# Two graph layers on one core: the order of the steps from a list scheduler in the kernel's text in place of a table of offsets

## The chip, the core and the metric

The kernel runs on one core of a Trainium2 chip. Its time is the device time of one execution in microseconds (us), as the median of several runs. The core has TensorE (PE: matmuls; PEld is its weight load), VectorE (DVE), ScalarE (ACT), GpSimd (POOL) and SyncE (SP, which here only issues transfers). Every engine takes its own instructions strictly in the order in which the program lists them; semaphores make it wait for others. Sixteen DMA engines carry the transfers that SP and ACT issue.

## The reference

128 graphs of 128 nodes with 512 features go through two layers, each with a residual. All is float32.

```python
def _layernorm(x, axis=-1, eps=1e-5): ...
# layer 0: h = relu(layernorm(x)); x = x + GAT(h, adj)
feats = jnp.einsum('bnf,hfu->bhnu', X, W)              # 8 heads of 64
e_self, e_neigh = ...                                   # feats . a_self, feats . a_neigh
dense = leaky_relu(e_self[..., :, None] + e_neigh[..., None, :], 0.2)
dense = dense + NEG_BIG * (1.0 - A[:, None, :, :])
att = softmax(dense); out = relu(att @ feats + b)
# layer 1: h = relu(layernorm(x)); x = x + HG(h, adj)
#   hypergraph_conv: H = (adj != 0); out = Dn * (H @ (Be * (H^T @ (x @ W^T)))) + b
h1 = relu(hypergraph_conv(x, adj, W1, b1))              # 512 -> 1024
y = hypergraph_conv(layer_norm(h1, gamma, beta), adj, W2, b2) + x    # 1024 -> 512
```

## The kernel before

Work is cut into **steps**, each a Python function that issues a few instructions on one engine. Attention and the first product with the graph's matrix go graph by graph (`parts`); the two dense products of layer 1 go by pairs of graphs (`second`), since each takes seven half-size products in place of eight (u1 to u7 and v1 to v7, with sums us1..4, vs1..4 of halves on POOL, L789 to L837).

A graph's path: x.load (SP), statistics and relu (DVE, POOL, ACT: L433 to L462), a transposition `x`, features `f` (PE, L578), neighbour scores sent to DRAM and fetched back as a broadcast (`ed`, L618 to L636), leaky, mask, row maximum and exponentials (`sc`, `pp`, L638 to L670), a transposition `p`, `av` (PE, L672), `oT` (ACT, L686), a transposition `o`, scaling and addition (L695 to L707), again statistics and relu (`h1`), `z` (PE, L714), `zT` (ACT). Then for the pair: u products into PSUM banks ux and uy, kept by DVE into aL, aR, bL, bR (L840 to L873), relu into `r`, statistics (L751, `sq`), a transposition `r`, v products into vx and vy, kept by DVE into `v`, and for each graph `y` (PE, L918), `y.keep` (DVE, L925, writes xt) and the store.

A **transposition** takes three steps. `send` (L472) is a transfer from ACT's queue to DRAM, `fetch` (L481) four transfers on SP's queue back in blocks (tiles xm, pm, om, rm), and `turn` (L494) one DVE transpose of 32 x 32 blocks (L509). In the first graphs (`DIRECT`: 4 of x, p, o, 2 of r) it is four or eight PE transposes into a PSUM bank and a copy instead (L502 to L507).

What sets the **order**: `Order` (L150) holds every step at a place, and `issue` calls them sorted by it. The place is `origin(n) + AT[step] - sooner`: AT gives each step an offset, origin goes up by STEP = 19.25 per graph after the eight rows of EARLY, and EARLY and LATE move groups of steps of the first eight and last six graphs. W2_AT places the setup steps (weights, bias rows, sums of weight blocks). For instance `ra.fetch` is at 130.27, `ra.turn` at 133.81, `u7.keep` at 99.35 of the next pair (137.85 on the same scale), `u4` at 99.48.

Each tile comes from a pool with a number of buffers per tag. PSUM has 8 banks: two shared "ps" (z, av, k, y), two for f, one each ux, uy, vx, vy. SBUF tiles with one buffer are xn, hT, pp, pT, oT, o, h1; xt has 12.

Of the kernel before, what the change touches and what calls it, by code (L numbers as in the profile page):

```python
# [13 lines left out]
P = 128  # L14
# [7 lines left out]
STEP = 19.25  # L22
EARLY = (
    (0, 3.05, 1.85, 0.05, 1.85, 1.85, 1.53, 1.85, -6.41),
    (19.25, 0, 0.01, -0.36, -0.36, -0.36, -0.36, -0.36, -1.29),
    (39.4, 0, -3.95, 0, 0, 12.9, 12.9, 12.9, 17.9),
    (57.75, 0, 0, 0, 0.34, 0, 0, 0, 0),
    (77.73, 0, 0, 0, 0, -4.29, -4.29, -4.29, -4.29),
    (96.25, 0, -2.95, 0, 0, 0, 0.05, 0, 0),
    (115.45, 0, 0, 0, 0, 0, 10.16, 11.08, 11.08),  # L30
    (134.75, 0, 24.41, 0, 0, 0, 0, 0, 0),
)
LATE = (
    (0, 0, 0, 0, 1.89, 0, 0, 0),
    (0, 0, 0, 0, 0, 0, 0, 0),
    (0.25, 0, 0, 1.08, 1.08, 1.08, 1.08, 0.74),
    (0, 0.14, 0.14, 0.14, 0.26, 0.14, 0.14, 0.14),
    (0, 0, 0, 0, -0.72, 0.07, -0.72, 0.34),
    (0, 3.7, 0, 0, 0, 0, -3.96, -3.96),
)  # L40
AT = {
    "x.load": -19.25,
    "x.stats": -15.55,
    "x.mean": -14.6,
    "x.rstd": -14.03,
    "x.relu": -13.05,
    "x.send": -12.05,
    "x.fetch": -9.3,
    "x.turn": -3.58,
    "f": 0,  # L50
    "e": 2.18,
    "f.keep": 5.65,
    "e.send": 4.8,
    "e.fetch": 8.85,
    "d.leaky": 11.65,
    "d.leaky1": 12.71,
    "d.mask": 12.49,
    "d.mask1": 14.25,
    "d.max": 14.4,
    "d.max1": 15.7,  # L60
    "d.exp": 15.25,
    "d.exp1": 17.1,
    "p.send": 19.43,
    "p.fetch": 24.45,
    "p.turn": 29.56,
    "av": 33.41,
    "av.keep": 34.48,
    "o.send": 39.2,
    "o.fetch": 51.02,
    "o.turn": 55.26,  # L70
    "o.scale": 56.16,
    "o.add": 56.52,
    "h.stats": 58.76,
    "h.mean": 59.09,
    "h.rstd": 59.72,
    "h.relu": 62.32,
    "z": 71.55,
    "z.keep": 78.03,
    "h.add": 64.28,
    "mask.load": -17.62,  # L80
    "mask": -12.02,
    "adj.load": 25.02,
    "adj.turn": 29.78,
    "adj.weigh": 31.52,
    "k": 40.72,
    "k.keep": 42.52,
    "k.deg": 43.62,
    "us1": 80.14,
    "us2": 83.46,
    "us3": 86.28,  # L90
    "us4": 91.36,
    "u1": 81.64,
    "u1.keep": 84.95,
    "u6": 86.88,
    "u6.keep": 88.66,
    "u2": 88.99,
    "u2.keep": 91.33,
    "r.aL": 96.5,
    "u5": 94.53,
    "u7": 92.8,  # L100
    "u7.keep": 99.35,
    "r.bR": 101.65,
    "u4": 99.48,
    "u4.keep": 104,
    "r.bL": 106.21,
    "u3": 100.3,
    "u3.keep": 102.03,
    "r.aR": 102.79,
    "rb.send": 110.98,
    "rb.stats": 119.65,  # L110
    "rb.root": 125.09,
    "rb.fetch": 114.54,
    "rb.turn": 119.23,
    "ra.send": 107.42,
    "ra.stats": 126.05,
    "ra.root": 128.88,
    "ra.fetch": 130.27,
    "ra.turn": 133.81,
    "vs1": 123.44,
    "vs2": 138.14,  # L120
    "vs3": 137.02,
    "vs4": 154.95,
    "v1": 142.38,
    "v1.keep": 145.34,
    "a1": 146.75,
    "b1": 150.3,
    "b0": 152.19,
    "v6": 144,
    "v6.keep": 147.65,
    "v2": 146.6,  # L130
    "v2.keep": 149.75,
    "v5": 150.87,
    "v7": 149.88,
    "v7.keep": 152.5,
    "v4": 159.95,
    "v4.keep": 162.65,
    "v3": 161.6,
    "v3.keep": 163.6,
    "ya": 164.91,
    "ya.keep": 166.04,  # L140
    "ya.store": 169.02,
    "yb": 183.16,
    "yb.keep": 186.01,
    "yb.store": 186.48,
}
W2_AT = (36.61, 3.95, -8.22, 41.62, 45.15, 53.53, 54.68, 1.33, 71.89, 0.13, 2.77, 7.82, -19.26, -18.51, 0.66, 4.2, -4.88, -5.39)
DIRECT = {"x": 4, "p": 4, "o": 4, "r": 2}


class Order:  # L150

    def __init__(self):
        self.todo = []

    def at(self, place, fn, *args):
        self.todo.append((round(place, 3), len(self.todo), fn, args))

    def issue(self):  # L160
        for _, _, fn, args in sorted(self.todo, key=lambda t: t[:2]):
            fn(*args)
# [3 lines left out]
def gat_then_hypergraph_kernel(  # L166
# [31 lines left out]
    io = ctx.enter_context(tc.tile_pool(name="io", bufs=12))  # L198
    wk = ctx.enter_context(tc.tile_pool(name="wk", bufs=2))
    dr = ctx.enter_context(tc.tile_pool(name="dr", bufs=2, space=bass.MemoryType.DRAM))  # L200
    gp = ctx.enter_context(tc.tile_pool(name="gp", bufs=2))
    sm = ctx.enter_context(tc.tile_pool(name="sm", bufs=4))
    ps = ctx.enter_context(tc.tile_pool(name="ps", bufs=2, space=bass.MemoryType.PSUM))
    pv = ctx.enter_context(tc.tile_pool(name="pv", bufs=1, space=bass.MemoryType.PSUM))
    pa = ctx.enter_context(tc.tile_pool(name="pa", bufs=1, space=bass.MemoryType.PSUM))
    ctx.enter_context(tc.manual_schedule())

    def psum(name):
        return ps.tile([P, 512], F32, tag="ps", name=name)

    def psum2(name):
        return pa.tile([P, 2, 512], F32, tag="pa", name=name)

    def psum_sums(tag, name):
        return pv.tile([P, 512], F32, tag=tag, name=name)

# [6 lines left out]
    nc.gpsimd.memset(eps_col, EPS)  # L223

    S = [dict() for _ in range(N)]
    SP = [dict() for _ in range(N // G)]

    def load_x(n):
        S[n]["xt"] = io.tile([P, F], F32, tag="xt", name=f"xt_{n}")
        nc.sync.dma_start(S[n]["xt"], x[n])  # L230

    def load_mask(g):
        s = SP[g]
        s["at"] = gp.tile([P, G, P], F32, tag="at", name=f"at_{g}")
        nc.sync.dma_start(s["at"], adj[g * G : (g + 1) * G].rearrange("n c e -> c n e"))

    def load_adj(g):
        s = SP[g]
        pair = adj[g * G : (g + 1) * G]
        s["am"] = gp.tile([P, G * NB, B], F32, tag="am", name=f"am_{g}")  # L240
        for b in range(NB):
            nc.sync.dma_start(
                s["am"][b * B : (b + 1) * B],
                pair[:, :, b * B : (b + 1) * B].rearrange("n (a x) y -> x (n a) y", x=B),
            )

        s["hmb"] = gp.tile([P, G, P + 1], F32, tag="hmb", name=f"hmb_{g}")
        nc.sync.dma_start(s["hmb"][:, :, P], pair[:, 0, :].rearrange("n e -> e n"))

    t1, t2, t4 = (const.tile([P, KP, FV], F32, name=f"w2_t{i}") for i in (1, 2, 4))
    gb = const.tile([2 * KH, P], F32, name="gb")
    rows = {}
    for key, v, tile_, at in (
        ("a_self", a_self, t1, 0),
        ("a_neigh", a_neigh, t1, F),
        ("b0", b0, t2, 0),
        ("b2", b2, t2, F),
        ("b1", b1, t4, 0),  # L260
    ):
        flat = v.rearrange("h u -> (h u)") if len(v.shape) == 2 else v
        row = tile_[0:1].rearrange("o k c -> o (k c)")
        rows[key] = row[:, at : at + flat.shape[0]]
        nc.scalar.dma_start(rows[key], flat.unsqueeze(0))
    w0_sb = const.tile([P, KF, 2, FB + E], F32, name="w0_sb")
    we_sb = const.tile([P, KF, 2, E], F32, name="we_sb")
    w1_sb = const.tile([P, KF, DH], F32, name="w1_sb")
    w2_sb = const.tile([P, KH, F], F32, name="w2_sb")

    def load_w0(k):
        for b in range(2):
            nc.sync.dma_start(
                w0_sb[:, k, b, 0:FB].rearrange("p (h u) -> p h u", h=HB),
                w0[b * HB : (b + 1) * HB, k * P : (k + 1) * P, :].rearrange(
                    "h p u -> p h u"
                ),
            )

    def load_w1():  # L280
        sw["w1"] = True
        nc.sync.dma_start(w1_sb, w1t.rearrange("(k p) h -> p k h", p=P))

    def load_w2():
        sw["w2"] = True
        nc.sync.dma_start(gb[0:KH], gamma.rearrange("(k p) -> k p", p=P))
        nc.sync.dma_start(gb[KH : 2 * KH], beta.rearrange("(k p) -> k p", p=P))
        nc.sync.dma_start(w2_sb, w2t.rearrange("(k p) o -> p k o", p=P))

    sw = {}  # L290
    ones = const.tile([1, P], F32, name="ones")
    nc.vector.memset(ones, 1.0)
    b0_bc = const.tile([P, F], F32, name="b0_bc")
    b1_bc = const.tile([P, DH], F32, name="b1_bc")
    b2_bc = const.tile([P, F], F32, name="b2_bc")
    bw_bc = const.tile([P, F], F32, name="bw_bc")
    gbT = const.tile([P, 2 * KH], F32, name="gbT")
    a_bc = [psum_sums(tag, f"a_bc_{tag}") for tag in ("ux", "vx")]
# [479 lines left out]

# [405 lines left out]
```

## Time and profile before

| what | value |
|---|---|
| time, median of 3 runs (lowest, highest) | 2631.27 us (2630.47, 2631.73) |
| profiled execution: its span, the only time the page gives of it | 2656.0 us, 24.7 above the median |
| DMA | 553.44 MB, 208 GB/s; 16 engines busy 73% in the middle |
| PE idle 0 to 200 us, 200 to 2550, 2550 to 2656 | 59.0, 92.8, 11.6 us |
| k of pair 3, k of pair 63 (PE) | 180.47, 2554.76 us |
| u1 of pair 0; last f | 119.84; 2535.44 to 2539 us |
| transfers, median from issue to landing | xm 3.1, pm 2.9, om 2.0, rm 3.0, sc 3.8 us |

A profile line of instructions reads: line and engine, operation, out<-in by the program's names, count; then busy us and ns of one; then the engine's idle time just before and what ended it. A line of waits reads: who waited for whom, us in all, times, longest. The busy row has one digit for each fortieth of the span, 9 for 90% or more; PEclk is the clock granted to TensorE in tenths. A timeline row begins with its start and its length.

### The profile page before, as it was taken

To read this page: it belongs to the slowest core of one execution; us is meant where nothing else is said; L and a number is where in the kernel's file an instruction comes from. 1 tells how busy PE (TensorE), PEld (TensorE's weight loads), DVE (VectorE), ACT (ScalarE), POOL (GpSimd) and SP (SyncE) were. 2 spreads that over 40 slices of the span, in tenths; PEclk is the share of its full clock that TensorE was granted. 3 is DMA by queue.
4 is the path that set the end of the run, shared out by engine and by line. 5 is a ranking of instruction groups with operands and counts; after the bars stand their busy time and mean duration, and the time that the engine had idled before them with its cause. 6 is when DMAs were issued, how large, how long until landed. Compare 5 with 4: busy or idle time off the path is not lost. (4 is left out here: it accounts for less than half of the span.)

```text
span 2656.0 us, 41199 instructions
## 1 busy us (share of the span) xinstructions
PE 2492.6 (94%) x11137; PEld 1752.2 (66%) x11137; DVE 1841.8 (69%) x3545; ACT 1664.3 (63%) x5455; POOL 1865.5 (70%) x2324
## 2 busy tenths in 40 slices
PE   6689999999999999999999999999999999999998
PEld 3456776676676676666666676666676676667666
DVE  3557777777777766767777677767777776767763
ACT  3466666666666666666666666666666666666652
POOL 3667777777777667777777777767777677777763
PEclk8799999999999999999999999999999999999999
DMA  4257776777777777676776777777777777777752
GB/s 132 80 162 214 224 230 213 220 228 221 219 226 222 215 218 213 209 230 207 215 235 212 213 233 221 219 218 225 217 223 223 217 222 220 217 220 226 218 167 91
DMA packets 559699, 553.44 MB, mean 208 GB/s; under 512 B 157269, under 2 KB 428645, under 8 KB 559466
## 3 DMA queue, kind: packets, MB, share of 16 engines
q1 hardware_dynamic: 487744, 354.68, 48.9%
q10 hardware_dynamic: 71722, 196.13, 19.1%
q8 instruction: 88, 1.44, 0.2%
q14 instruction: 145, 1.19, 0.2%
HBM read 318.85 MB, written 231.74 MB: 207 GB/s over the span
## 5 line engine op out<-in xcount | busy, mean ns | idle before, releaser
L589 PE MATMUL f<-w_sb,hT 128*128 128x264 f32 (+1 forms) x2048 | 491.6, 395 | 24.0 <-DVE hT L509 15.3
L589 PEld LDWEIGHTS f<-w_sb,hT 128*128 128x128 f32 x2048 | 397.6, 195 | 122.3 <-issue 31.2
L643 ACT ACTIVATE sc<-sc,es 128x128 f32<-128x128 f32 x1024 | 318.9, 391 | 146.8 <-DMA sc<-ed 135.1
L648 POOL TENSOR_TENSOR sc<-sc,at 128x512 f32<-128x512 f32 x256 | 322.8, 1272 | 121.9 <-ACT sc L643 120.2
L662 ACT ACTIVATE pp<-sc,nmx 128x128 f32<-128x128 f32 x1024 | 395.9, 390 | 15.1 <-DVE nmx L653 10.0
L704 POOL TENSOR_TENSOR xt<-xt,o 128x512 f32<-128x512 f32 x128 | 163.2, 1275 | 324.0 <-DVE o L700 324.0
L457 ACT ACTIVATE xn<-xt,nmr_a,rstd_a 128x512 f32<-128x512 f32 x128 | 104.2, 814 | 305.9 <-POOL nmr_a L452 290.6
L653 DVE TENSOR_REDUCE nmx<-sc 128x4 f32<-128x512 f32 x256 | 173.0, 676 | 144.3 <-POOL sc L648 141.0
L830 PEld LDWEIGHTS vx<-w_sb,rT 128*128 128x128 f32 x1024 | 194.4, 190 | 83.6 <-issue 46.3
L830 PE MATMUL vx<-w_sb,rT 128*128 128x256 f32 x1024 | 242.1, 379 | 2.5 <-DVE rT L509 2.4
L830 PE MATMUL ux<-w_sb,zT 128*128 128x512 f32 x512 | 241.6, 594 | 0.0
L662 ACT ACTIVATION_READ_ACCUMULATOR pp<-sc,nmx 128x1 f32 x1024 | 193.6, 189 | 0.0
L761 ACT ACTIVATE sq<-r,nm 128x512 f32<-128x512 f32 x256 | 182.7, 714 | 4.2
L678 PE MATMUL av<-pT,feats 128*64 128x128 f32 x2048 | 142.3, 281 | 42.2 <-DVE xt L928 31.5
L830 PE MATMUL uy<-w_t,zT 128*128 128x512 f32 x256 | 128.9, 627 | 53.9 <-DVE bR L841 53.9
L509 DVE STREAM_TRANSPOSE pT<-pm 128x1024 f32<-128x1024 f32 x124 | 153.7, 1240 | 30.9 <-DMA pm<-pd 30.1
L689 ACT ACTIVATE oT<-av 128x512 f32<-128x512 f32 x128 | 75.1, 586 | 155.3 <-PE av L678 154.6
L509 DVE STREAM_TRANSPOSE rT<-rm 128x1024 f32<-128x1024 f32 x126 | 155.7, 1236 | 23.2 <-DMA rm<-rd 22.4
L736 POOL TENSOR_TENSOR xt<-xt,b_bc 128x512 f32<-128x512 f32 x128 | 163.7, 1279 | 10.0
L735 POOL TENSOR_TENSOR xt<-xt,h 128x512 f32<-128x512 f32 x128 | 163.2, 1275 | 1.3 <-ACT h L457 1.3
L928 DVE SCALAR_TENSOR_TENSOR xt<-y,dn,xt 128x512 f32<-128x512 f32 x128 | 95.6, 747 | 96.3 <-PE y L921 96.0
L509 DVE STREAM_TRANSPOSE hT<-xm 128x512 f32<-128x512 f32 x124 | 87.8, 708 | 106.8 <-DMA xm<-xd 106.6
(155 smaller groups left out, 5728.1 us busy)
## 6 DMA issues: line engine op xcount, KB each, us to landing
sc<-ed SPq DMA_DIRECT2D x256, 256.0 KB, 3.8
rd<-r ACTq DMA_DIRECT2D x126, 512.0 KB, 3.5
rm<-rd SPq DMA_DIRECT2D x504, 128.0 KB, 3.0
pd<-pp ACTq DMA_DIRECT2D x124, 512.0 KB, 2.9
pm<-pd SPq DMA_DIRECT2D x496, 128.0 KB, 2.9
xt<-in_x SPq DMA_DIRECT2D x128, 256.0 KB, 4.7
out<-xt SPq DMA_DIRECT2D x128, 256.0 KB, 2.3
xd<-xn ACTq DMA_DIRECT2D x124, 256.0 KB
```

The source lines that it names most:

```text
L509: nc.vector.transpose(S[n][tag].rearrange("p k (a x) -> p k a x", x=B), S[n].pop(key + "m").rearrange("p a (k y) -> p k a y", y=B),)
L589: nc.tensor.matmul(s["f"][:, b, cols], hT[:, k, :], weights[:, k, b, :], start=(k == 0), stop=(k == KF - 1),)
L643: nc.scalar.activation(sc, sc, AF.Prelu, bias=s["es"][:, h : h + 1], alpha=SLOPE)
L648: nc.gpsimd.tensor_tensor(sc, sc, neg.to_broadcast([P, HB, P]), ALU.add)
L653: nc.vector.tensor_reduce(s["nmx", part], s["sc"][part], AX.X, ALU.max, negate=True)
L662: nc.scalar.activation(blocks(n, "p", s["pp"])[:, h], s["sc"][part][:, j].rearrange("p (b y) -> p b y", y=B), AF.Exp, bias=s["nmx", part][ ...
L678: nc.tensor.matmul(s["av"][side * U : (side + 1) * U, j * P : (j + 1) * P], feats[n % NF][:, h * U : (h + 1) * U], pT[:, h, :], start=True ...
L704: nc.gpsimd.tensor_tensor(s["xt"], s["xt"], s.pop("o").rearrange("p k c -> p (k c)"), ALU.add)
L735: nc.gpsimd.tensor_tensor(s["xt"], s["xt"], s["h1"], ALU.add)
L736: nc.gpsimd.tensor_tensor(s["xt"], s["xt"], b2_bc, ALU.add)
L761: nc.scalar.activation(sq, s["r"][:, q * 512 : (q + 1) * 512], AF.Square, bias=nm[:, 1:2], accum_out=ss[:, q : q + 1],)
L830: nc.tensor.matmul(p[w + bank][:, 0:cols], left[:, k, :], right[:, k, :], start=(first and k == 0), stop=(k == kb - 1), skip_group_check=n ...
```

## The change

The table and `Order` go. Each step becomes a `Step` with an engine, a duration in ns (`took`), the steps it comes after, the slots that it uses and, for transfers, the time it occupies the DMA engines (`work`). `rank` gives each step the earliest place at which its chain of predecessors in the same pair could have it done, counted from 19000 ns times the graph, plus a constant from RANK for its key. `lay_out` then goes through time: for each engine it finds the steps whose predecessors are placed and for whose new tiles a slot is open, takes from those that could start within LOOK of the soonest the one with the lowest rank, and places the engine's step that starts first. Steps of one key stay in the order of the graphs. A tile's slot is the one that opened longest ago; it opens when the last of its users ends. All steps are then issued by start.

The setup steps (loads of w0, w1, w2, score columns, bias rows, sums of blocks) are in the same list; their temporary tiles take zT slots. The score columns are reduced straight into w0_sb (before: into we_sb, copied by `join_weights`, L328). The direct transposes use the ps banks (before vx and vy). Row statistics lie in one 12-wide tile; `sq` has a buffer of its own (before it shared tag "a" with aL). Numbers of buffers and banks are otherwise those of before; the instructions of a step, their engines and shapes too.

```diff
-STEP = 19.25
-EARLY = (
-    (0, 3.05, 1.85, 0.05, 1.85, 1.85, 1.53, 1.85, -6.41),
...
-AT = {
-    "x.load": -19.25,
...
+LOOK = {"PE": 200, "DVE": 150, "ACT": 150, "POOL": 150, "SP": 0}
+TAIL = {"PE": 165, "DVE": 85, "ACT": 95, "POOL": 45, "SP": 0}
+REACH = {"PE": 160, "DVE": 50, "ACT": 50, "POOL": 80, "SP": 60}
+AGAIN = {"PE": -165, "DVE": 35, "ACT": 35, "POOL": 90, "SP": 0}
+DMA_HEAD, DMA_FOOT = 1300, 700
+PERIOD = 19000
+DIRECT = {"x": 4, "p": 4, "o": 4, "r": 2}
+SLOTS = {
+    "xt": 12, "at": 2, "am": 2, "hmb": 2, "hmT": 1, "kk": 5, "dn": 8, "xn": 1, "xm": 1, "hT": 1,
+    "feats": 3, "sc": 3, "pp": 1, "pm": 1, "pT": 1, "oT": 1, "om": 1, "o": 1, "h1": 1, "zT": 3,
...
+    "ps": 2, "f": 1, "ux": 1, "uy": 1, "vx": 1, "vy": 1,
...
+RANK = {
+    "a1": 3890, "adj.load": 100333, "adj.turn": 122866, "adj.weigh": 94622, "av": -5583, "av.keep": -181780,
...
+    "r.fetch": 109999, "r.pe0": -88117, "r.pe1": 53012, "r.root": -52723, "r.send": 15648, "r.stats": 44523,
+    "r.turn": 88847, "rows": 55300, "score.copy": -141112, "score.p0": -5102, "score.p1": -21697, "score.rows": 57189,
+    "score.s0": -78925, "score.s1": -22941, "u1": 12006, "u1.keep": 73574, "u2": -130042, "u2.keep": -277853,
...
+    "u7": -1510, "u7.keep": -26096, "us1": -65977, "us2": -90890, "us3": -104222, "us4": -15425, "v1": -225017,
+    "v1.keep": -43082, "v2": -102297, "v2.keep": 160590, "v3": -73291, "v3.keep": 38041, "v4": -201075,
+    "v4.keep": -1574, "v5": -9218, "v6": 19043, "v6.keep": -50666, "v7": -133739, "v7.keep": 29565, "vs1": -25369,
...
+    def lay_out(self):
...
+                for s in ready[e]:
+                    at = max(at_e, s.ready)
+                    for tag, _ in s.takes:
+                        opens = min((t for t in slots[tag] if t is not None), default=None)
+                        if opens is None:
+                            at = None
+                            break
+                        at = max(at, opens + REACH[e])
...
+                at, s = min((x for x in found if x[0] <= soonest + LOOK[e]), key=lambda x: (x[1].rank, x[1].order))
+                if best is None or at < best[0]:
+                    best = at, s
...
+            s.start = at
+            free[e] = at + s.took
+            if s.work:
+                dma_free = max(at + DMA_HEAD, dma_free) + s.work
+                s.end = dma_free + DMA_FOOT
+            else:
+                s.end = at + s.took + TAIL[e]
...
+        add(f"{key}.send", n, "ACT", 330, made, [rows, d], work=(720, 1280)[k // 8])
+        add(f"{key}.fetch", n, "SP", 1900, [(f"{key}.send", n)], [d, m], work=(1120, 1700)[k // 8])
+        add(f"{key}.turn", n, "DVE", (625, 1155)[k // 8], [(f"{key}.fetch", n)], [m, (tag, n)])
...
+        add("u7", g, "PE", 1716, [("us3", g), ("u6.keep", g)], [zb, y])
+        add("u5", g, "PE", 1716, [("us1", g), ("u2.keep", g)], [s1, z])
+        add("u7.keep", g, "DVE", 1310, [("u7", g), ("u5", g)], [y, z, bR, ("dn", g)])
+        add("u4", g, "PE", 1716, [("u7.keep", g)], [zb, y])
...
+    with tc.manual_schedule():
+        for s in order:
+            run[s.key](s.i)
```

## The prediction

> **What bounds the kernel now.** I read the page's busy shares first, then the waits of TensorE, then two stretches of the timeline, then the rows of the first 125 us.
>
> ```profile
> span 2656.0 us, 41199 instructions
> PE 2492.6 (94%) x11137; PEld 1752.2 (66%) x11137; DVE 1841.8 (69%) x3545; ACT 1664.3 (63%) x5455; POOL 1865.5 (70%) x2324
> PE   6689999999999999999999999999999999999998
> PEclk8799999999999999999999999999999999999999
> ```
>
> TensorE is the bound: busy 94% of the span, every other engine 63 to 70%, the DMA engines 73% between 200 and 2550 us. What an order can change is the 163.4 us in which PE is idle, and the clock. The windows view splits the idle time: 59.0 us before 200 us, 92.8 us from 200 to 2550 (2350.0 less 2257.18 busy), 11.6 us after.
>
> ```profile
> PE uy L830 <- DVE bR L841: 53.9, 63, 2.6
> PE av L678 <- DVE xt L928: 31.5, 27, 1.7
> PE f L589 <- DVE hT L509: 15.3, 6, 5.3
> PE uy L830 <- POOL us L806: 14.3, 17, 2.7
> ```
>
> Of the middle's 92.8 us, 49.3 belong to the first line (59 waits, once per pair), 31.5 to the second, 10.7 to the fourth. The timeline shows what the first is made of (PE, then DVE):
>
> ```profile
> 1049.46 0.61 PE L545 MATMUL k<-hmb,hmT 128*128 128x129 f32 x4
> 1052.63 2.55 PE L830 MATMUL uy<-w_t,zT 128*128 128x512 f32 x4 [2.56 <-DVE bR L841]
> 1054.97 3.06 PE L830 MATMUL uz<-w_sb,us 128*128 128x512 f32 x4
> ```
>
> ```profile
> 1049.80 1.25 DVE L509 STREAM_TRANSPOSE rT<-rm 128x1024 f32<-128x1024 f32 x1 [2.16 <-DMA rm<-rd]
> 1050.97 0.65 DVE L436 BATCH_NORM_STATS2 st_b<-xt 128x6 f32<-128x512 f32 x1
> 1051.65 0.18 DVE L441 BATCH_NORM_AGGREGATE mv_b<-st_b 128x2 f32<-128x6 f32 x1
> ```
>
> DVE stood at the head of its queue waiting for a transfer (rm), and behind that wait stood bR (u7.keep), which u4 on PE needs. The table has `ra.fetch` at 130.27 and `ra.turn` at 133.81, 3.54 apart; four fetches take 1.85 us to issue and land 3.0 us later, 4.85 in all. So the table was short by about 1.3 us at this place.
>
> The price per pair of graphs: k, the one PE step that comes once per pair, starts at 180.47 and sixty pairs later at 2554.76, so 39.57 us a pair. The pair from 654.52 to 692.90 took 38.38 with 0.50 of idle in it: 37.88 us is what its instructions need. So 1.69 us a pair can go, 1.55 of it idle and the rest slow clock: 60 x 1.69 = 101 us at most. The stretch before 180.47 and the 101.2 us after 2554.76 are the other two terms.
>
> On the clock: the two matmul groups above took 2.55 and 3.06 us where the same groups take 1.98 and 1.88 elsewhere, right after a 2.56 us wait; the granted clock was 0.83, 0.76, 0.83 and 0.93 in the first four 50 us windows, and f took 5.8 to 6.2 us there against 3.72 later. The Trainium skill ("TensorE: Matmul & The Clock Gate", Part 1) has the half clock come after about 3.4 us of idle; this trace shows one after 2.56. By the page such a wait would cost its own length, by the trace 1.8 us more; the granted clock read 0.99 in two of the nine 200 us windows from 400 to 2200 us and 1.00 in the others, so the sum below doesn't need it.
>
> **The change, part by part.** *Work removed or added.* Almost none: the same matmuls, activations, sums and transfers. Setup writes the score columns straight into w0, which takes away one 0.18 us copy on DVE; sq gets a buffer apart from aL; the small statistics of a row lie in one tile. The transposes of the first graphs move from banks vx/vy to the two shared ps banks. All this is off the path, at nothing; at worst the 20 bank uses of the direct transposes wait for one another at 0.7 us each (a DVE copy from PSUM, 0.67 to 0.69 us), 14 us, all in a stretch where PE idles anyway.
>
> *The middle part.* The order is now worked out event by event: an engine takes, among steps that could start within 150 ns (200 on PE) of the earliest possible, the lowest rank, and it knows when a slot opens. Two kinds of stall are of the sort that this sees. av behind the ps bank that y.keep frees (31.5 us): another ready product goes first. uy behind POOL us (10.7): likewise. The third kind (49.3 us) it sees only as well as it knows when a transfer lands, since DVE still takes its turns in order. Its figures for r: 1.3 head + 1.7 + 0.7 foot = 3.7 us from the issue on idle DMA engines; the rows give 4.85. For x: 3.1 against 1.85 + 3.1 = 4.95; for p: 3.7 against 1.85 + 2.9 = 4.75; for o: 3.1 against 1.85 + 2.0 = 3.85. It is short by 0.75 to 1.85 us, made up in part because it lets transfers queue one behind the other. A case worked out: in the stall above xm, om and rm were issued at 1039.59, 1041.48 and 1043.44; by its figures rm lands at 1047.1, in the trace DVE had it at 1049.80, 2.7 later. So I let the first two kinds go for the most part and the third stay: best case all 1.69 us a pair, worst case a stall longer than now (priced as a rival). I take 0.65 us a pair, near the 42.2 us of the first two kinds over 60 pairs (0.70): 60 x 0.65 = **-39 us**.
>
> The Trainium skill ("DMA: Bandwidth & Descriptors", Issuing engines are not separate DMA queues) speaks against the change here: transfers of all issuers interleave on the same 16 engines, so a short one is held up by a long one beside it, where the plan serves them one after another. If every landing came late in that way, the rival of late landings below would be the forecast.
>
> *The head.* The rows show work waiting in queues whose order was fixed: graph 0's oT was written at 49.95 (0.57 us), its transposes ran on PE at 68.82, behind f of graph 2 (6.02 us), the 7.03 us of sw_ps and others. z of graphs 0 and 1 ran at 80.37 and 104.54, u1 of pair 0 at 119.84. From rows of graph 0, f ends at 25.86 and its last exponential at 38.40, 12.5 us; then transposes 1.04, copy 0.67, av 1.09, oT 0.57, transposes 0.6, copy 0.69, scaling 0.88, add 1.28, statistics 0.87, root 1.1, h 0.81, z 1.05, zT 0.58: 11.2, and some 2 of hand-overs. So graph 1, whose f ended at 41.8, could have zT at 67.5 and u1 begin 52 us sooner. The two f and the z and av that now run ahead of it would run behind it (2 x 3.7 at full clock, and about 6 more): 14 us of the 52 come back. Best -38, worst 0 (the setup steps and the single slots of hT, pT, o and h1 hold it back); I take two thirds, **-25 us**.
>
> *The tail.* Now the last f ends at 2539 and PE still has 113 us of stored-up work, nearly without gaps. An order that prefers the late steps (RANK puts v1, v4 and u2 ahead by 225, 201 and 130 us) stores up less. The last pair's chain would then show: r 0.63, rd 3.5, fetch 4.85, turn 1.25, some 10 us; the chain from f to zT, 24 us, at worst with half of it covered by the pair before. Ends: -5 and +25. I take **+9 us**, the nearer to the first of these chains.
>
> Sum: -39 - 25 + 9 = -55 us, against the profiled execution's span of 2656.0; that span is 24.7 us above the median of the runs, 2631.27, and I take the difference over unchanged: 2631 - 55 = **2576 us**, 2.1% faster.
>
> **Rivals.**
> 1. *Late landings become the bound (slower).* Place: DVE's queue, whose turns (hT, pT, o, rT: eight a pair) are now put at the moment the plan thinks a transfer lands. For it: the shortfall above, and that DVE already waits 106.6 us for xm, 40.7 for om, 30.1 for pm, 22.4 for rm, beside 1841.8 us busy. Against it: DVE has some 5 us free per graph, and most steps behind a turn aren't what PE needs next. Price: one more wait of 1 us a pair ahead of a keep that PE needs: pair 40.6, +62, and -25 + 9 elsewhere: 2677. It decides from 0.27 us a pair more than now on (16 us over 60 pairs), i.e. PE idle above 1.8 us a pair in the middle.
> 2. *Only the head gains.* The stalls of the middle move to other steps with the same sum: -25 + 9: 2615. For it: PE has run at 96% there, and every step has a single slot in one place or another (hT, pT, o, h1, ux, uy, vx, vy).
> 3. *Nearly all stalls go.* -101 - 38 + 9: 2501. For it: other engines have 28% free. Against it: the third kind of stall.
> 4. *The plan gives much the same order.* 2631.
>
> **How the numbers follow.** Forecast 0.46, rival 1 0.28, rival 2 0.14, rival 3 0.08, rival 4 0.04. What a measurement of this kernel can tell from no change is 0.2%, 5 us. Faster: 0.46 + 0.08 + 0.12 of rival 2 = 0.66; same: 0.04 + 0.02 = 0.06; slower 0.28. The range reaches from 2530 (leaves out most of rival 3, 0.06) to 2680 (leaves out about half of rival 1, 0.14). The forecast's own range, with the middle's gain between 20 and 70 us and the other two terms as taken, is 2545 to 2595.
>
> **What would show it.** Right: pairs (k to k) of 38.9 us on the mean, PE idle of about 55 us in the middle, av<-xt and uy<-us all but gone from PE's waits; u1 of pair 0 before 95 us; PE idle after the last f above 20 us. Wrong: PE's longest wait on a DVE step that stands behind a turn, with DVE's waits for xm, om, pm, rm well above 200 us in all (rival 1); the same sum of PE idle in the middle under other names (rival 2); u1 still near 120 us would undo the head's term.

## The result and the profile after

The changed kernel takes 2809.33 us (median of 4 runs, 2805.08 to 2815.95) against 2631.28 us (2630.47 to 2631.73): a ratio of 1.0685, 95% interval 1.0663 to 1.0708. It is slower, on the side of rival 1 (2677 us), and by more than that rival was priced at.

The page of the kernel after, the same four rows that were shown of before:

```profile
span 2814.2 us, 41024 instructions
PE 2552.1 (91%) x11137; PEld 1761.6 (63%) x11137; DVE 1882.9 (67%) x3544; ACT 1669.6 (59%) x5455; POOL 1903.2 (68%) x2324
PE   7899999999899998999898988999989889899998
PEclk8999999999999999999999999999999999999999
```

PE fills up sooner (7899 at the start, 6689 before), but from there on single 8s stand where before had only 9s. With the same 11137 matmuls it is busy 59.6 us longer and idle 98.6 us longer; together 158.2 us, the difference of the two spans. (The medians differ by 178.1: the profiled execution of before was 24.7 us above its median, that of after lies 4.9 above.)

Cut at k of pair 3 and k of pair 63, as in the prediction: k of pair 3 comes at 94.9 us (180.47 before), the sixty pairs take 2555.4 us (2374.3 before), what follows 163.9 (101.2). So head and tail together gain 22.9 us and **the middle loses 181.1 us, 3.02 a pair** (42.59 for 39.57). The windows view of the middle, after first, then before; the columns are the stretch, its length, busy time and matmuls of PE, then PEld, DVE, ACT and POOL, the granted clock, the DMA share and GB/s:

```profile
200.00:2700.00 2500.00, 2279.80 (x10012) 1582.08 (x10011) 1692.15 (x3189) 1504.99 (x4933) 1704.20 (x2089) 0.98 0.67 203
```

```profile
200.00:2550.00 2350.00, 2257.18 (x10189) 1596.03 (x10187) 1695.26 (x3263) 1532.55 (x5036) 1702.74 (x2136) 1.00 0.72 220
```

PE idles 220.2 us of 2500 (92.8 of 2350 before), at a clock of 0.98 in place of 1.00. The DMA share fell from 0.72 to 0.67: the DMA engines do the same work in more time, so they aren't used up.

Who waits, in the kernel after, first PE, then DVE, then ACT (us in all, times, longest):

```profile
PE vx L903 <- DVE dn L738: 118.7, 58, 3.6
PE vx L903 <- ACT b L973: 68.2, 42, 2.7
PE vy L903 <- DVE a L983: 12.4, 21, 1.5
...
PE ps L818 <- DVE xt L1004: 4.0, 9, 0.7
```

```profile
DVE st_a L627 <- DMA xt<-in_x: 149.3, 107, 3.2
DVE rT L684 <- DMA rm<-rd: 142.5, 73, 4.8
...
DVE o L684 <- DMA om<-od: 111.2, 108, 2.5
```

```profile
ACT sc L791 <- DMA sc<-ed: 234.4, 94, 7.9
ACT sc L791 <- DMA om<-od: 192.6, 34, 7.3
```

ACT stands idle 427 us by these two rows ahead of its work on the scores (in all 34 waits of the second an xd send stands in its queue just before); v1.keep stands in the same queue and comes 4.5 us after v1 (1.94 in the plan), which is PE's second row. Of three of the waits that the prediction began with little is left: uy behind bR (53.9) is 0.4 us now, av behind xt (31.5) is 4.0 (L818; its bank is called ps here), and uy behind us (14.3) is no longer among the rows. In place of these stands one wait per pair, v1 (vx) behind DVE. It names dn, a small step; the timeline shows what DVE had stood in front of. PE, DVE and SP of the kernel after:

```profile
1013.36 3.73 PE L745 MATMUL f<-w_sb,hT 128*128 128x264 f32 x16
1019.39 3.09 PE L903 MATMUL vx<-w_sb,rT 128*128 128x256 f32 x8 [2.31 <-DVE dn L738]
1022.27 2.52 PE L903 MATMUL ux<-w_sb,zT 128*128 128x512 f32 x4
```

```profile
1014.70 0.74 DVE L919 SCALAR_TENSOR_TENSOR bL<-ux,dn,b_bc 128x512 f32<-128x512 f32 x1
1018.09 1.25 DVE L684 STREAM_TRANSPOSE rT<-rm 128x1024 f32<-128x1024 f32 x1 [2.66 <-DMA rm<-rd]
1019.26 0.12 DVE L738 TENSOR_SCALAR dn<-ps 128x2 f32<-128x2 f32 x1
```

```profile
1011.07 3.65 SPq L677 DMA_DIRECT2D rm<-rd  x4
1015.80 2.84 SPq L677 DMA_DIRECT2D xm<-xd  x4
```

DVE was done at 1015.43 and waited 2.66 us for rm, whose four transfers SP had begun to issue at 1011.07 and took 3.65 us to issue; v1 needs the rT that DVE then makes. It is the shape of the stall in before (a turn at the head of DVE's queue, its transfer not landed), with v1 now directly behind it. DVE's longest row of waits is one that the prediction priced nowhere, the load of x: 41.0 us before, 149.3 now. That load lands 4.2 us after its issue in both kernels (median), and the plan reckons with 2.7; no experiment below takes it by itself.

Two numbers set the scale. By the plan's own arithmetic, which `lay_out` leaves in its steps, the 128 graphs end at 2468.9 us, 37.41 a pair, with PE idle for 12.9 us after 200 us and for none from 200 to 2300. On r's path it leaves little: for the first graph of a pair it puts the turn 0.7 us after the landing that it reckons with (3.8 us after the first issue), and v1 1.4 us after the turn's end. And in the plan v1 starts 15.52 us after u3 of its pair (about 42 us in the table of before: 100.3 to 142.38), on the chip 18.2; from v1 to the next u3 it is 21.9 planned and 24.8 measured. r's whole round trip lies in the first of the two.

### The profile page after: what moved, and what is told of

Read it like the earlier page. It is cut to its first block, busy times and chain, and to the rows that moved or that the text cites. A ratio compares the mean times of both kernels' runs of the same rounds, so it can differ in the third digit from the quotient of the medians.

```text
span 2814.2 us, 41024 instructions
## 1 busy us (share of the span) xinstructions
PE 2552.1 (91%) x11137; PEld 1761.6 (63%) x11137; DVE 1882.9 (67%) x3544; ACT 1669.6 (59%) x5455; POOL 1903.2 (68%) x2324
## 4 chain that ended last, share of the span: by engine, by line
DMA 27%; ACT 18%; PE 18%; POOL 11%; issue 9%; DVE 7%; SPq 6%; ACTq 1%; DVEq 0%; POOLq 0%
DMA rm<-rd 9%; ACT pp L806 6%; PE vx L903 5%; PE uy L903 5%; SPq L677 5%; DMA sc<-ed 4%; PE vy L903 4%; DMA pd<-pp 4%; DMA rd<-r 4%; ACT sq L960 3%; POOL sc L796 3%; DVE rT L684 3%; PE ux L903 2%; ACT sc L791 2%; POOL rT L884 2%
## 5 line engine op out<-in xcount | busy, mean ns | idle before, releaser
L903 PE MATMUL vx<-w_sb,rT 128*128 128x256 f32 x1536 | 415.4, 418 | 198.1 <-DVE dn L738 118.7
L903 PEld LDWEIGHTS vx<-w_sb,rT 128*128 128x128 f32 x1536 | 307.3, 206 | 312.8 <-DVE dn L738 142.8
L745 PEld LDWEIGHTS f<-w_sb,hT 128*128 128x128 f32 x2064 | 390.3, 192 | 91.8 <-issue 28.8
L903 PE MATMUL ux<-w_sb,zT 128*128 128x512 f32 x512 | 258.5, 629 | 7.2 <-ACT zT L858 4.6
L968 POOL TENSOR_TENSOR rstdc<-ss,neghalf 128x1 f32<-128x1 f32 x128 | 74.2, 580 | 262.8 <-ACT ss L964 262.8
L684 DVE STREAM_TRANSPOSE rT<-rm 128x1024 f32<-128x1024 f32 x126 | 156.3, 1240 | 142.9 <-DMA rm<-rd 142.5
L976 POOL TENSOR_TENSOR b<-b,bw_bc 128x256 f32<-128x256 f32 x128 | 113.3, 885 | 161.2 <-ACT b L973 160.8
L960 ACT ACTIVATE sq<-r,ss 128x512 f32<-128x512 f32 x256 | 184.8, 722 | 8.3
L627 DVE BATCH_NORM_STATS2 st_a<-xt 128x6 f32<-128x512 f32 x128 | 88.6, 692 | 149.3 <-DMA xt<-in_x 149.3
L638 ACT ACTIVATE xn<-xt,st_a 128x512 f32<-128x512 f32 x128 | 103.2, 807 | 120.3 <-POOL st_a L634 113.6
L684 DVE STREAM_TRANSPOSE o<-om 128x512 f32<-128x512 f32 x124 | 88.1, 711 | 111.4 <-DMA om<-od 111.2
L884 POOL TENSOR_TENSOR vs<-rT 128x512 f32<-128x512 f32 x64 | 81.7, 1276 | 118.8 <-DVE es L767 112.9
```

Source lines behind the costliest of these rows:

```text
L684: nc.vector.transpose(T(to, n).rearrange("p k (a x) -> p k a x", x=B), T(key + "m", n).rearrange("p a (k y) -> p k a y", y=B),)
L745: nc.tensor.matmul(T("f", n)[:, b, cols], T("hT", n)[:, k, :], w0_sb[:, k, b, cols], start=(k == 0), stop=(k == KF - 1),)
L903: nc.tensor.matmul(bank(w, g, which)[:, 0:cols], left[:, k, :], right[:, k, :], start=(first and k == 0), stop=(k == kb - 1), skip_group_c ...
L960: nc.scalar.activation(sq, T("r", n)[:, q * 512 : (q + 1) * 512], AF.Square, bias=ss[:, 5:6], accum_out=ss[:, q : q + 1])
```

## The experiments

Pairs are counted in this part from y of pair 3 to y of pair 59 on PE (of the second graph of each): 43.01 us in the change, 39.60 in before. "Issue to landing" is the median in the middle, per fetch, from SP's first of its transfers to the landing of the last one. Kernels with a single run are compared by their pairs and by differences of tens of us.

### Waits between transfers: more DRAM slots, another merge of the queues

ACT's xd send waited 168.5 us in all in the middle for one of two DRAM buffers. Six each for xd, pd, od, rd, ed:

```diff
-        tiles[tag] = [pool.tile(SHAPES[tag], F32, name=f"{tag}_{i}") for i in range(n)]
+        tiles[tag] = [pool.tile(SHAPES[tag], F32, name=f"{tag}_{i}") for i in range(6 if tag in IN_DRAM else n)]
```

> Six DRAM buffers in place of two for each round trip, order unchanged on every engine. Takes away one wait alone: x.send of graph n, on ACT, for x.fetch of graph n-2; in the changed kernel ACT stood 1.57 us per xd send in it (168.5 us in the middle), and v1.keep stands behind it. If that wait is what stretches v1 to v1.keep (4.48 us against 1.94 in the plan), the pair falls from 42.9 us by up to 2.5 us and the time from 2809 to about 2650. If late landings as such, or the completion of the transfer eight places ahead in the list, set the pace, the send waits for the next of these almost as long and the time falls by less than 40 us.

Measured 2812.30 us, 42.93 a pair. The xd send's issue to landing fell from 3.76 to 2.41 us, but no pair got shorter: that wait wasn't what set the pair.

Each engine's order kept, the common list merged by the measured starts:

```diff
-    order = plan.lay_out()
+    laid = plan.lay_out()
+    queues = {e: iter([s for s in laid if s.engine == e]) for e in LOOK}
+    order = [next(queues[{"P": "PE", "D": "DVE", "A": "ACT", "G": "POOL", "S": "SP"}[c]]) for c in MERGE]
```

> Every engine's own order and every slot as in the changed kernel; only how the five lists are merged into one differs: by the starts measured on the chip and not by the plan's. That alters which earlier transfer a transfer has to see completed before it is issued (each waits for the one eight places ahead in the merged list; 161 of 499 transfers from ACT get another). If ACT's transfers waiting on SP transfers that run late is a main cost, the time falls by 50 to 150 us; if the order on each engine and the landing times make the loop, it stays within 30 us of 2809.

Measured 2813.31 us, 42.94 a pair. This run says nothing on its question: the waits it was to move hardly moved. Gaps in SP's issuing that end just as an ACT transfer with the same completion semaphore lands add up to 209.2 us in the change (200 to 2500 us) and 200.5 here.

### What a fetch costs: bytes, count, and which fetch

One transfer of the four (r, x, p and o alike), the rest of xm, pm, om, rm set to a constant once:

```diff
-            for b in range(NB):
+            for b in range(1):
```

> Leaves work out: each fetch moves the first of its four blocks only (the turned tiles hold stale blocks), so SP issues 1 transfer in place of 4, a quarter of the fetched bytes moves, and a quarter of the completions is waited for. Order and slots unchanged. If the transfers (landing, SP's queue, completions) are the whole of the loss, the pair falls from 42.9 to near the 37.9 us that the instructions need, and the time to 2480 to 2530. If the engines' own order (DVE, ACT, POOL queues) makes the loop, the pair stays above 40.5 and the time above 2650.

Four transfers, each with a quarter of its bytes:

```diff
-                    T(key + "m", n)[b * B : (b + 1) * B],
-                    T(key + "d", n)[:, b, :].rearrange("(a x) r -> x a r", x=B),
+                    T(key + "m", n)[b * B : (b + 1) * B, 0:1],
+                    T(key + "d", n)[0:B, b, :].rearrange("(a x) r -> x a r", x=B),
```

> Each fetch keeps its four transfers, but each moves only a quarter of its block (the rest of xm, pm, om, rm holds a constant; the output is not the reference's). Theory A, the time that the bytes take to land is what delays the turns: near the run with one transfer per fetch (2502 us, 37.84 a pair), 2500 to 2580 us. Theory B, the count of issues on SP's queue and of completions to be waited for is what delays: no better than about 2760 us, over 42 us a pair. Both in parts: between, and the place between 2502 and 2809 gives the shares.

Only r, and only the others:

```diff
-            for b in range(NB):
+            for b in range(1 if key == "r" else NB):
```

> Only the fetch of r moves one block of four (the rest of rm holds a constant; the output is not the reference's); x, p and o are fetched whole. Theory A, the loop u3, r.send, r.fetch, r.turn, v1, u3 of the next pair sets the pair: this run alone takes away more than half of the loss against the run with all four quartered (307 us), so below 2655 us and under 40.4 us a pair. Theory C, the fetches load the queues and whichever lands late stalls the order, r no more than the others: r is a third of the fetched bytes (512 of 1536 KB per graph), so about 100 us of the 307, 2700 us or more.

```diff
-            for b in range(NB):
+            for b in range(NB if key == "r" else 1):
```

> The complement: fetches of x, p and o move one block of four, that of r all four (constants in the rest; the output is not the reference's). Theory A: although two thirds of the fetched bytes have three quarters taken away, less than half of the loss goes, 2655 us or more, unless r itself lands sooner because the queue ahead of it is shorter. Theory C: about 200 of the 307 us go, 2600 us or less.

All bytes in one transfer, to other places and other partitions (the m tiles one element wider per block so that rows stay as short):

```diff
-            for b in range(NB):
-                nc.sync.dma_start(
-                    T(key + "m", n)[b * B : (b + 1) * B],
-                    T(key + "d", n)[:, b, :].rearrange("(a x) r -> x a r", x=B),
-                )
+            d = T(key + "d", n)
+            nc.sync.dma_start(T(key + "m", n)[:, :, 0 : d.shape[2]], d)
```

> Each fetch is one transfer in place of four, with the same bytes in rows of the same length (1 KB for r and p, 512 bytes for x and o), but not to the places that the turn needs, so the output is not the reference's. The complement of the run in which four transfers moved a quarter each (2531 us). Theory B, the count has a part of its own: SP issues a fetch in 0.4 us in place of 1.9, and the eight completion semaphores that SP's and ACT's transfers share in rotation come round half as often (in the change, gaps of SP that end as an ACT transfer with the same semaphore lands add up to 209 us between 200 and 2500 us): 2690 to 2760 us, about 41.4 a pair. Theory A alone, only the bytes delay: 2790 us or more.

| kernel | time | a pair | issue to landing of r, p, o, x |
|---|---|---|---|
| the change | 2809.33 | 43.01 | 5.85, 6.11, 5.76, 4.34 |
| one transfer of four, all fetches | 2502.15 | 37.84 | 2.48, 2.64, 2.66, 2.22 |
| four transfers, a quarter of the bytes | 2530.66 | 38.28 | 3.12, 3.94, 4.26, 3.97 |
| one transfer of four, r only | 2614.63 | 39.71 | 3.15, 5.86, 5.78, 5.00 |
| one transfer of four, x, p, o only | 2532.30 | 38.26 | 4.25, 2.83, 2.96, 3.00 |
| one transfer, all bytes | 2622.76 | 39.77 | 4.51, 5.79, 3.80, 4.11 |

The fetches are the whole excess over the plan: without three quarters of them a pair takes 37.84 us, 0.43 above the plan's own 37.41. The same edit was not tried on the kernel before; there it could gain 1.9 us a pair at most (39.60 less the 37.7 for which PE is busy per pair in this run), so at least 3.2 of the 5.17 belong to the new order. How the excess is made up went against most expectations. The bytes alone bring 4.73 us a pair of the 5.17, as theory A said; but one transfer in place of four, with all bytes, brings 3.24, more than theory B had expected (2622.76 for 2690 to 2760). r alone brings 3.30, again as A said and not C; x, p and o alone bring 4.75, which A allowed only if r itself then landed sooner. It did, and that is what all five share: r, the transfer behind which v1 stands, lands 1.3 us sooner or more (4.51 and below, for 5.85), in two of them without a change of r's bytes, by a shorter issue or by a shorter queue ahead of it. The parts add up to far more than the whole. Cut at v1 and v2, the pair shows why (mean of pairs 4 to 58, us; the plan's from its own arithmetic):

| kernel | u3 to v1 | v1 to v2 | v2 to the next u3 |
|---|---|---|---|
| the plan of the change | 15.52 | 3.44 | 18.45 |
| the change | 18.17 | 5.53 | 19.26 |
| one transfer of four, all fetches | 15.80 | 3.45 | 18.51 |
| one transfer of four, r only | 16.31 | 3.87 | 19.47 |
| one transfer of four, x, p, o only | 15.93 | 3.61 | 18.65 |
| one transfer, all bytes | 16.80 | 3.93 | 18.97 |

The change loses 2.7 us ahead of v1, behind r's turn, then 2.1 between v1 and v2, where PE waits for v1.keep in ACT's queue, and 0.8 in the rest. So the lateness enters a pair more than once, and each of the edits shortens both of the first two stretches. With r alone, r lands 2.7 us sooner and the pair is 3.3 us shorter. The run with one transfer can't be read as 1.3 us of r for 3.2 us of a pair, since o lands 2.0 us sooner in it too.

### Telling the plan that fetches land later

```diff
-                s.end = dma_free + DMA_FOOT
+                s.end = dma_free + DMA_FOOT + 1700 * s.key.endswith(".fetch")
```

> The plan is told that a fetch lands 1.7 us later (measured: 1.0 to 2.3 us later than it reckons); everything else, RANK too, as in the changed kernel. If wrong landing times alone spoil a sound method, the pair falls below 40.5 us and the time below 2690. If RANK's constants only suit the timetable for which they were found, the new order is poor by its own reckoning (39.0 us a pair in place of 37.4) and the time stays within 60 us of 2809.

Measured 2897.44 us, 44.34 a pair, slower. The plan itself then has 39.0 us a pair, and the chip adds 5.3 to it, as much as to the plan of the change (5.6). It is outside both of the ranges expected. From u3 to v1 there are 24.5 us on the chip now (18.2 in the change), and that alone didn't help. RANK's constants were kept; that they suit only the timetable for which they were found fits the plan's own 39.0 for 37.41, and does not explain the 5.3.

### The half clock

In the pair shown v1 took 3.09 us behind its wait and the next group 2.52, where the same groups take 1.99 and 1.88 elsewhere: 1.7 us. It is not so in every pair. Of v1's 44 waits of more than 1.5 us (pairs 1 to 62), 23 were followed by a v1 of over 2.3 us, the others by one of 2.0 us, as in the next pair:

```profile
1062.31 2.00 PE L903 MATMUL vx<-w_sb,rT 128*128 128x256 f32 x8 [2.23 <-DVE dn L738]
```

In all PE is busy 59.6 us longer than before, some 1 us a pair. Whether that is part of the loss was tried with matmuls that need nothing of rT, put ahead of v1 into the bank that it overwrites; eight, then four:

```diff
+        if (w, i) == ("v", 1):
+            for _ in range(8):
+                nc.tensor.matmul(T("vx", (g, "x"))[:, 0:FV], w2_sb[:, 0, 0:P], w2_sb[:, 0, 0:FV], start=True, stop=True)
```

> Eight matmuls of 128x256 on w2 go ahead of v1 of every pair, into the bank that v1 then overwrites: 1.9 us of PE work at the place where PE waits 118.7 us in 58 waits, 2.0 us each. They need nothing of rT, so they run in the wait. If the half clock after such waits is a cost of its own (PE busy was 60 us higher than in before): the wait falls by about its whole length, v1 runs at the full clock, and the time falls by 20 to 50 us against 2809. If the clock is only a sign of the wait: 2809 within 10 us, or later by the pairs in which v1 had no wait (two of 60).

> Four matmuls of 128x256 go ahead of v1 of every pair in place of the eight of the run before, which took 3.5 us, some 1.5 us longer than the wait that they stood in (2.0 us), gave the clock 0.995 in place of 0.973, and left the pair at 42.93 us. Four take 1.8 us, less than the wait. Theory D, the half clock after v1's wait lies on the path (v1 3.09 us and the next group 2.52 where they else take 1.99 and 1.88, 1.7 us a pair): the pair falls by 1 to 1.7 us, to 2710 to 2755 us. Theory E, the loop is bound by the landing and PE's slow matmuls only fill time that would be waited: 2800 us or more.

Measured 2818.05 and 2813.44 us, 42.93 and 42.96 a pair, at a mean clock of 0.995 and 0.990 for 0.973. PE's longest waits with the four matmuls:

```profile
PE vx L906 <- ACT b L976: 89.7, 57, 2.8
PE vx L906 <- DVE dn L738: 26.3, 31, 1.7
```

The wait behind DVE fell from 118.7 to 26.3 us, no v1 took over 2.3 us any more, and the pair stayed. With four matmuls v1 starts as late as before (18.2 us after u3), v2 comes 0.3 us sooner behind it, held by v1.keep (89.7 us of waits for 68.2), and the rest of the pair is 0.2 us longer. With eight, 3.5 us of work a pair were added (their expectation had put it at 1.9) and the pair stayed as well. So theory D (1 to 1.7 us a pair, from the one pair shown) is refuted and E holds: PE has time to spare in this order, and the half clock was a sign of the waits, not a cost on top of the pair. I had counted its 60 us as a part of the loss until then.

### Other numbers in the same scheduler

Only RANK's constants and a landing time by kind of transfer differ; they were sought off the chip with landings, and the waits between transfers, as the traces show them.

```diff
+FOOT = {
+    "adj.load": 9971, "e.fetch0": 2660, "e.fetch1": 1475, "e.send": 1575, "mask.load": 7184, "o.fetch": 2342,
...
+}
...
-                s.end = dma_free + DMA_FOOT
+                s.end = dma_free + FOOT.get(s.key, DMA_FOOT)
```

> The scheduler, its steps and slots stay; only numbers change: all constants of RANK, and the time from the end of a transfer to its landing by kind of transfer (0.34 to 11.9 us, for the fetches 2.3 to 5.9, in place of 0.7 for all). They were sought against landings as the runs show them (r.fetch 5.9 us from issue to landing, p.fetch 6.1, o.fetch 5.7, a transfer waiting for the one eight before) in place of the plan's own. In the plan v1 now stands 28.8 us behind u3 of its pair (15.5 in the change; about 42 in the table of before), at the same 37.5 us a pair. Theory A, a landing loop without slack made the change slow: with the slack the pair is 37.5 to 38.5 us and the time 2490 to 2560, below both kernels. Rival F, a list scheduler with these steps can't hold its timetable on the chip whatever its numbers, since each late transfer shifts the engines' orders: 41 us a pair or more, above 2690. Rival G, DMA service is the floor (fetches alone have 91% of the loss): no pair below the 39.6 of before, about 2600 or more.

Measured 2626.9 us (10 runs), 0.9987 of before (0.9962 to 1.0013), 39.68 a pair. 182 us of the loss are gone with the scheduler, steps and slots unchanged, so rival F fell, but theory A's 37.5 to 38.5 was missed too, and rival G (a floor at 39.6) still stood. v1 no longer waits in the middle. One wait of PE is left, and the product that waits is v3, the last into bank vx, behind v7.keep on DVE; the timeline shows the old shape, a turn ahead of that keep. PE's row of waits, then PE, DVE and SP of this kernel:

```profile
PE vx L910 <- DVE v L990: 93.2, 54, 3.8
```

```profile
1047.76 1.97 PE L910 MATMUL vx<-w_sb,rT 128*128 128x256 f32 x8 [1.87 <-DVE v L990]
```

```profile
1044.83 1.25 DVE L691 STREAM_TRANSPOSE rT<-rm 128x1024 f32<-128x1024 f32 x1 [1.79 <-DMA rm<-rd]
...
1047.13 0.48 DVE L990 SCALAR_TENSOR_TENSOR v<-vx,rstdc,b 128x256 f32<-128x256 f32 x1
```

```profile
1031.24 5.66 SPq L708 DMA_DIRECT2D am<-in_adj  x4
...
1038.81 2.00 SPq L684 DMA_DIRECT2D rm<-rd  x4
```

The four am transfers took 5.66 us to issue. The trace names a completion semaphore for every transfer, eight in all, each used 441 or 442 times by SP and ACT together, and the fourth am transfer went out at 1036.59, 0.02 us after a transfer of r by ACT with the same semaphore had landed (1036.57). Such gaps of SP add up to 758 us here, 209 in the change, 80 in before. The next numbers were sought with these waits as the built program has them:

> Again only the constants of RANK and the times from a transfer's end to its landing differ from the change; in the plan v1 stands 28.8 us behind u3 as in the replan before, at the same 37.5 us a pair. They were chosen so that SP's transfers seldom share a completion semaphore with a send of ACT that is still to come: in the replan before, SP's gaps that end as such a send lands were 758 us of 972 (80 of 895 in before), and its pair was 39.68. Theory H, the shared completions held that replan at 39.7: the pair is 37.8 to 38.8 us, the time 2520 to 2595, and those gaps of SP are below 300 us. Rival G, the service of the DMA engines or the scheduler is the floor at about 39.6 a pair: 2610 us or more, whatever becomes of those gaps.

Measured **2573.45 us** (6 runs, 2567.40 to 2577.77), 0.9783 of before (0.9756 to 0.9811), 38.94 a pair: faster than both kernels, though the interval leaves open whether by 2%. The page:

```profile
span 2576.0 us, 41054 instructions
PE 2465.9 (96%) x11137; PEld 1747.1 (68%) x11137; DVE 1833.6 (71%) x3544; ACT 1686.7 (65%) x5455; POOL 1878.5 (73%) x2324
PE   5899999999999999999999999999999999999998
PEclk9999999999999999999999999999999999999999
```

Rival G fell. Theory H was right on the time (2520 to 2595), just missed the pair (38.8), and was wrong on its sign: SP's gaps behind ACT's transfers are 770 us, not below 300. So it was not the sum of SP's waits that was mended; whether it was their place, and which of them no longer reach PE, wasn't taken apart.

Both replans put 28.8 us between u3 and v1 in the plan, for 15.5. Whether that distance took r's round trip off the loop was asked by the two quartering edits on the second replan (the diffs as above):

> The second replan (2573 us, 38.94 us a pair) with the fetch of r moving one block of four, the rest of rm a constant; the output is not the reference's. In the change the same edit took 3.3 us off a pair (43.01 to 39.71). If the distance of 28.8 us between u3 and v1 takes r's round trip off the loop: less than 0.8 us off a pair, 2525 us or more. If the replan is as sensitive to r as the change, only with less to gain: nearly all of the 1.4 us by which its pair exceeds the plan's 37.51, below 2500 us.

> The second replan with the fetches of x, p and o moving one block of four, constants in the rest; the output is not the reference's. In the change this took 4.75 us off a pair. What is left of the replan's excess over its plan (1.4 us a pair) should sit here if r is off the loop: 37.5 to 38.1 us a pair, 2480 to 2520 us. If neither this nor r alone brings a pair under 38.5, the rest is not the landing of the fetches at all.

Measured 2514.15 us, 37.82 a pair with r quartered; 2522.34 us, 38.01 with x, p and o. PE's longest wait but for the start, in the second replan and then with r quartered:

```profile
PE vx L910 <- DVE v L990: 61.9, 59, 2.5
```

```profile
PE vx L914 <- DVE v L994: 3.9, 8, 1.3
```

```profile
PE vx L914 <- DVE v L994: 14.5, 17, 1.5
```

The last row is that with x, p and o quartered. Quartering r takes 1.12 us of the replan's 1.43 over its plan, between the two expectations and above the 0.8 that the distance theory allowed; quartering x, p and o takes 0.93, a pair as expected (37.5 to 38.1) at a time just past its range. Either edit removes most of the excess, so they overlap. The one run of the kernel before beside these two took 2655.86 us, 28 us above its median beside the replan, so the two may read some us long. The distance did take r off v1's path: v1 does not wait, and starts 2.2 us after the end of its turn. But r's turn still holds up DVE's queue, and v7.keep behind it reaches PE at v3 (1.1 us a pair, 0.2 with r quartered). SP's gaps behind ACT's transfers don't set the pair: with x, p and o quartered none are left, with r quartered 438 us, and the second has the shorter pair. Which property of the new numbers brought the 4.1 us a pair stays open; shown is that it lies in the numbers, and that what is left is again the landing of the fetches.

## Why the prediction was wrong, point by point

**Where the time can change.** "What an order can change is the 163.4 us in which PE is idle, and the clock" bounded the gain, and the second replan took 53 us of it (110.1 us of PE idle are left). For a loss there was no bound: the new order added 98.6 us of idle time.

**The middle, -39 us: the step that failed.** It read "I take 0.65 us a pair, near the 42.2 us of the first two kinds over 60 pairs". These two kinds did go, as argued (31.5 us to 4.0, and no row for uy behind us), and the third, which was to stay, went too (53.9 us to 0.4). But the sum treated the rest of the order as unchanged, and put what new waits would cost at nothing. The new order moved v1 to 15.5 us behind u3 in its plan, and there r's landing came late: 2.7 us a pair above the plan ahead of v1, 2.1 more at v1.keep. Measured +3.02 us a pair against before, +181.1 us.

**Rival 1, 2677 us, had the mechanism and not the size.** Its place was DVE's turns, and that is where it happened: rT behind rm 22.4 to 142.5 us, o behind om 40.7 to 111.2 (hT behind xm, 106.6 before, has no row any more; the four together went from 200 to 272), PE's longest wait on a DVE step behind a turn, as "What would show it" had written under wrong. Its price, "one more wait of 1 us a pair", was the term that was too small: 3.02 us. The shortfall of the landing figures was in the text (0.75 to 1.85 us), and 2.7 us in the worked case. It was made one wait of 1 us because DVE had some time free. Two things were left out. In the new order r itself landed later than the rows of before gave, 5.85 us after its first issue for 4.85, so that it came 2.05 us after the plan's 3.8, as much as the 2.1 us that the plan has between that landing and v1 beside the turn; no run separates a longer issue on SP from the transfers beside it. And the lateness enters a pair again at v1.keep in ACT's queue. The plan's own figures would have told: 37.41 us a pair against the 37.88 which the prediction worked out for the instructions, with landings that the rows already showed to be 0.75 to 1.85 us short, should have made rival 1 the forecast. Tightness alone does not explain it, though: the plans of the two replans have 37.5 us a pair as well, with later landings, and the chip adds 2.2 and 1.4 us to them and not 5.6.

**The head, -25, and the tail, +9.** Together -16; measured -22.9. u1 of pair 0 came at 82.55 us (119.84; below 95 was the mark), and up to 200 us PE was busy 173.05 us, 32.1 more than before. From the end of the last f to the end of the span there are 119.9 us (116.8 before), so the tail is +3 and not +9, and PE idles 17.5 us in it, below the mark of 20; that leaves -26 for the head. So the head was right, and the tail was too large by 6 us.

**The clock, "the sum below doesn't need it".** Right, for a reason that I didn't have. A half clock did come, after waits of 2.31 us and the like, and PE was busy 59.6 us longer, but with it taken away the pair is the same. The Trainium skill ("TensorE: Matmul & The Clock Gate", Part 1) has it come after about 3.4 us of idle; the trace of after, like that of before, shows it sooner, behind some of v1's waits from 1.9 us on, and not behind others of up to 3.0 us.

**The difference of 24.7 us carried over unchanged.** It belonged to the one execution that was profiled: where a profiled execution's own time is on record, its span is within 2 us of it. One other execution of before was nearly as long (2655.86 us, beside the last two runs). It moved the forecast by nothing, since forecast and baseline shared it.

**The range, 2530 to 2680,** ended at rival 1's price, which had only its one value. A rival that is a loop without slack has no such end: its range should have reached to the landing shortfalls counted once per turn ahead of PE, several us a pair.

## What to carry to other kernels

An order that is worked out from a timetable is as good as its landing times, and a late transfer can cost more than its own lateness: here r's landing, 2.7 us sooner with a quarter of its bytes, made a pair 3.3 us shorter, ahead of v1 and again ahead of v2. Before building, hold the plan's own figures against issue-to-landing times from a trace, and ask how much time the plan leaves behind each of them; after building, quarter the transfers once to see how much of a pair is theirs. A longer busy time of TensorE, or a lower clock, may be an effect of waits: put idle work into the wait and see whether the time moves.

## What the runs showed of the hardware and was not expected

- In these programs all transfers of SP and ACT share eight completion semaphores in rotation (441 or 442 uses each), so a transfer of SP can wait for one of ACT that it has nothing to do with (758 us of SP's 972 us of gaps in the first replan, 80 of 895 in before).
- A fetch of 512 KB in four transfers takes 5.85 us from its first issue to its last landing in the change, the same bytes in one transfer 4.51 us, a quarter of them in four transfers 3.12 (each in a run of its own, with the other fetches changed in the same way).
- Eight extra matmuls of 128x256 per pair (3.5 us, 8% of a pair) on the engine that is 91% busy cost nothing that could be seen (42.93 us a pair for 43.01).
